# Query, key and value by seven block products instead of eight, with x parked in HBM and variances on ScalarE

## The chip, the cores and the metric

The kernel runs on one core of one Trainium2 chip. The metric is the device time of one execution in microseconds; the time before is the median of four runs, 3240.68 us (3240.06 to 3242.31).

## The reference, cut to what matters

Four graph layers work on `x` of shape (128, 128, 512): 128 batches of 128 nodes with 512 features, float32 throughout, with one weighted adjacency `adj` of 128 x 128. After each layer comes a residual addition and a normalisation over the features.

```python
x = layernorm(x + gnn0(x))   # (adj @ x) @ w0 + bias0
x = layernorm(x + gnn1(x))   # graph attention: h = x @ W, softmax(leaky(s1 + s2) * adj) @ h, elu
x = layernorm(x + gnn2(x))   # max over neighbours' features: relu(max(adj @ x) + b)
x = layernorm(x + gnn3(x))   # masked 8-head attention on x @ w_qkv, projection, o + layernorm(o)*gamma + beta
```

In layer 3 the queries, keys and values are `x @ w_qkv`, a 512 x 1536 product for each batch. `layernorm` has no gain of its own: (x - mean) / sqrt(var + 1e-5).

## The kernel before, in words

One batch is a tile `x` of 128 nodes (partitions) by 512 features. `batch(i)` is a generator that takes batch i through all four layers; each `yield use(engine, time, buffers)` asks a planner for an engine and for buffers, and the instructions that follow it are put into the program at that point. The planner (`Plan`) runs all chains against one another with estimated durations and fixes the order of the instructions on every engine: among requests that can start first it takes urgent ones, then the lowest rank, which is mostly the batch's number. It ends with the order; on the chip each engine runs its instructions in that order and waits on semaphores. PE requests that aren't urgent are planned up to 1 us after their inputs are ready (`MARGIN`).

The batches form groups: two pairs at the start, 28 groups of four, six pairs at the end. A group shares `xT` (its features transposed, 512 x up to 512 columns), `qkT` (queries and keys transposed, later the attention weights) and the layer 1 logits. Per batch, TensorE does:

- layer 0: `mixed_rows` (one 128x512 matmul with adj, L289) and `product` with w0 (four 128x512 matmuls, L262); the first 12 batches use `mixed` (L270)
- layer 1: `mixed` with the attention (L270) and `product` with W
- layer 2: one matmul with adj (L783)
- layer 3: `query_key` (L621) on the whole group's columns, `values` (a `product` into `v`, L262), `score` (L670, 64-row tiles, heads side by side), `attends` (L691), `product` with the projection (L262)

Each float32 matmul call becomes two instructions in the profile. `tiled` puts a group's scores and the attends of the group before it next to each other on PE; only the last groups have attends of their own (`attend`).

Transposes go through HBM: VectorE transposes 32x32 squares (L292, L798, L843), the SP queue writes them out (`to_squares`, `to_rows`) and reads them back in place (`from_squares`, `from_rows`); `features` brings a batch's columns into `xT` in this way. `layernorm_act` takes statistics on VectorE (`mean_rstd`: L191, L197, L199), the power -0.5 on GpSimd (`root`, L205) and applies it on ScalarE (L225); `layernorm_dve` applies it on VectorE (L230). `layernorm_sums` gets the mean from a sum that the operation before it left and the variance from a square with a sum on ScalarE (L239); only the last batch but one uses it. `pool_add` (L255) is an addition on GpSimd. `x` keeps its buffer, one of 19, from its load to the store of the result; PSUM has 8 banks (`ps`).

Of the kernel before, what the change touches and what calls it, by code (L numbers as in the profile page):

```python
# [8 lines left out]
F32 = mybir.dt.float32  # L9
AF = mybir.ActivationFunctionType  # L10
ALU = mybir.AluOpType
# [4 lines left out]
P = 128  # L16
D = 512
K = D // P
G = 4
FIRST, PAIRS = 2, 6  # L20
SOON = (0, 4, 0, 4, 10, 0)
WHOLE = 2
SCALED = 2
# [11 lines left out]
    "x": 19, "yT": 4, "z": 2, "e": 2, "et": 1, "eT": 2, "ex": 2, "xT": 2, "v": 7, "qkT": 2,  # L35
    "pt": 1, "xt": 2,
# [3 lines left out]
LATER = 18  # L40
LANDED = 4.0
MARGIN = 1.0
LAND, ROW_LAND = 2.0, 0.0053

# [96 lines left out]
def gnn_stack_kernel(  # L141
# [24 lines left out]
    one = ctx.enter_context(tc.tile_pool(name="one", bufs=1))  # L166
# [65 lines left out]
    def layernorm_sums(xb, total):  # L232
# [4 lines left out]
        b_sq = yield use("ACT", 1.2, "ex")  # L237
# [47 lines left out]
    def mixed_rows(xb, nodes):  # L285
# [4 lines left out]
        bt = yield use("DVE", 0.71, "xt", urgent=True)  # L290
# [59 lines left out]
    wqkv_sb = const.tile([P, K, 3 * D], F32, name="wqkv_sb")  # L350
    wproj_sb = const.tile([P, K, D], F32, name="wproj_sb")
# [11 lines left out]
    scalars_in, w0_in, w3_in, wa_ready = (Event() for _ in range(4))  # L363
# [16 lines left out]
    def loads():  # L380
# [44 lines left out]
        landing(w3_in, (4 * K + 3) * P)  # L425
        for i in range(12, NB):
            yield from load(i)
# [33 lines left out]

    def logit_rows(a_sb, slot):
# [3 lines left out]
        for s in range(2):  # L466
            for k in range(K):
                yield use("DVE", 0.8)
                scr = one.tile([P, D], F32, name="scr")
                nc.vector.scalar_tensor_tensor(  # L470
                    scr, w1_sb[:, k, :], 1.0, a_sb[:, s, :], op0=ALU.mult, op1=ALU.mult,
                    accum_out=wa[:, k, s : s + 1],
                )
        give(slot)
# [10 lines left out]
    class Group:  # L485


        def __init__(self, first, size):
            self.first, self.size = first, size
            self.chunks = D // (size * P)  # L490
# [3 lines left out]
            self.turned, self.qk = Event(size), Event(2 * K // self.chunks)  # L494
            self.rows, self.attended, self.scored = ([Event() for _ in range(size)] for _ in range(3))
            self.heads, self.o, self.sc = {}, {}, {}
            self.eT, self.xT, self.qkT, self.slot, self.left = {}, None, None, {}, {}
# [19 lines left out]
    def group(i):  # L517

        g = group_of[i]
        if g not in groups:  # L520
# [5 lines left out]
            steps = K // gr.chunks  # L526
            for n in range(2 * steps):
                plan.start(query_key(gr, n // 2 * gr.chunks + K * (n % 2)), rank + n / K)


            joined = len(sizes) - PAIRS
            if g < joined:
                plan.start(tiled(gr, groups.get(g - 1), range(size)), rank)
            else:
                plan.start(tiled(gr, None, range(size)), rank)
            if g >= joined - 1:
                for b in range(0, size, 2):
                    for bs in ((b, b + 1),) if g < len(sizes) - 1 else ((b,), (b + 1,)):
                        plan.start(attend(gr, bs), first)
# [3 lines left out]
    def attention1(gr, h):  # L543
# [5 lines left out]
        st = small.tile([P, 2, Q, S // Q], F32, name="s2")  # L549
# [58 lines left out]
    def query_key(gr, c):  # L608
        yield gr.turned
        yield w3_in  # L610
        got = yield use("PE", 3.44, lambda: ("ps",) if gr.qkT else ("ps", "qkT"), late=0.2)
        if gr.qkT is None:
            bp, gr.slot["qkT"] = got
            gr.qkT = buf(gr.slot["qkT"], G, 2 * K, P)
        else:
            bp = got
        n = gr.chunks
        p = bank(bp, n, gr.size * P)
        for j in range(n):
            for k in range(K):  # L620
                nc.tensor.matmul(  # L621
                    p[:, j, :], wqkv_sb[:, k, (c + j) * P : (c + j + 1) * P],
                    gr.xT[:, k, : gr.size * P], start=(k == 0), stop=(k == K - 1),
                )
        gr.read("xT", gr.size + 2 * K // n)
        yield use("ACT", 0.6, urgent=True)
        for j in range(n):
            dst = gr.qkT[:, : gr.size, c + j, :]
            if c < K:
                nc.scalar.mul(dst, p[:, j, :].rearrange("p (b n) -> p b n", b=gr.size), HD**-0.5)  # L630
            else:
                nc.scalar.copy(  # L632
                    dst.rearrange("p b (c r) -> p b c r", c=Q),
                    p[:, j, :].rearrange("p (b r c) -> p b c r", b=gr.size, c=Q),
                )
        give(bp)
        done(gr.qk)
# [46 lines left out]
    def attends(gr, bs, slots):  # L684
        for b, slot in zip(bs, slots):
            valued, prT = gr.heads.pop(b)

            p = bank(slot, K, P)
            for c in range(K):
                for j in range(2):  # L690
                    nc.tensor.matmul(  # L691
                        p[j * HD : (j + 1) * HD, c, :],
                        valued.v[:, (2 * c + j) * HD : (2 * c + j + 1) * HD],
# [3 lines left out]
            gr.o[b] = p, slot, valued  # L697
# [3 lines left out]
    def values(i, gr, event):  # L701
        b = i - gr.first
        yield gr.turned
        bp, bv = yield use("PE", 3.44, lambda: ("ps", "v"), late=0.2)
        p = product(
            bp, lambda k: gr.xT[:, k, b * P : (b + 1) * P], lambda k: wqkv_sb[:, k, 2 * D :]
        )
        yield use("ACT", 0.6, urgent=True)
        event.v = buf(bv, D)
        nc.scalar.copy(event.v, p)  # L710
        give(bp)
        gr.read("xT", gr.size + 2 * K // gr.chunks)
        event.slot = bv
        done(event)

    def features(xt, bt, gr, b):

        scratch = yield from to_squares(xt, bt)
# [287 lines left out]
```

## Time and profile before

| | |
|---|---|
| median of the runs | 3240.68 us |
| the profiled execution | 3240.78 us |
| its span | 3238.8 us, granted TensorE clock 0.999 |
| PE busy, instructions | 3225.0 us (100%), 12135 |
| DVE busy | 2627.0 us (81%) |
| ACT busy | 1183.1 us (37%) |
| POOL busy | 932.6 us (29%) |
| DMA | 366.15 MB, the SP queue's packets 39.6% of 16 engines' span |

PE is TensorE's matmuls, PEld its weight loads (they overlap), DVE is VectorE, ACT ScalarE, POOL GpSimd, SP the engine that issues the DMAs. Shares are of the span, first to last instruction; the time of the execution is 2.0 us longer. In groups of instructions, a group is a line, an operation and a tile, with count, busy time, mean length in ns, and the idle time before it with what ended that. "Busy" of pipelined matmuls counts overlapped time once, so it is the pitch from one to the next that is worked with, not the length of one.

### The profile page before, as it was taken

What the parts mean: (1) busy time and instruction counts of PE and PEld (TensorE: products, weight loads), DVE (VectorE), ACT (ScalarE), POOL (GpSimd) and SP (SyncE); (2) the same over time, 40 slices, a digit from 0 to 9 for tenths busy, and PEclk for the clock granted to TensorE, in tenths of its full rate; (3) what the DMA queues carried; (4) which work ended last, traced back from release to release, by engine and by line L of the source; (5) the groups of instructions that cost most, each with busy time, mean ns of one, the idle gap of its engine ahead of it and who ended that gap; (6) DMA issues with size and microseconds to landing.
All of it is one profiled execution on the core that took longest, in us unless ns stands there. A gap on an engine that the chain in (4) does not pass through costs nothing.

```text
span 3238.8 us, 40147 instructions
## 1 busy us (share of the span) xinstructions
PE 3225.0 (100%) x12135; PEld 1663.4 (51%) x12135; DVE 2627.0 (81%) x5649; ACT 1183.1 (37%) x3477; POOL 932.6 (29%) x1033
## 2 busy tenths in 40 slices
PE   9999999999999999999999999999999999999998
PEld 5654445545455454554544545545455454455565
DVE  7888777887878778888788787887878877888867
ACT  2444333333342333333334333343233332333432
POOL 3322222232332323323223232232322322323222
PEclk9999999999999999999999999999999999999999
DMA  6234333444334443344433444334443344442432
GB/s 217 77 103 120 108 97 93 135 122 127 87 93 134 123 127 99 88 129 120 128 96 91 127 122 129 108 78 124 123 128 111 87 110 129 127 121 71 126 89 98
DMA packets 732167, 366.15 MB, mean 113 GB/s; under 512 B 566192, under 2 KB 648496, under 8 KB 731952
## 3 DMA queue, kind: packets, MB, share of 16 engines
q1 hardware_dynamic: 731808, 363.33, 39.6%
q8 instruction: 97, 1.59, 0.2%
q14 instruction: 118, 0.97, 0.1%
q10 hardware_dynamic: 144, 0.26, 0.0%
HBM read 190.38 MB, written 173.08 MB: 112 GB/s over the span
## 4 chain that ended last, share of the span: by engine, by line
PE 98%; DVE 1%; DMA 1%; issue 0%; POOL 0%; SPq 0%; ACT 0%; POOLq 0%; DVEq 0%; ACTq 0%
PE ps L262 54%; PE ps L621 26%; PE ps L270 4%; PE ps L670 4%; PE ps L691 4%; PE ps L783 3%; PE ps L289 3%; DMA p_d<-pt 0%; DMA x_d<-xt 0%; DVE st L191 0%; PE ps L921 0%; DVE t L889 0%; DVE pt L843 0%; DMA yT<-x_d 0%; POOL rstd L205 0%
## 5 line engine op out<-in xcount | busy, mean ns | idle before, releaser
L621 PE MATMUL ps<-xT,wqkv_sb 128*128 128x512 f32 (+1 forms) x2304 | 886.0, 545 | 0.0
L205 POOL TENSOR_TENSOR rstd<-ve,neghalf 128x1 f32<-128x1 f32 x640 | 437.1, 683 | 1486.5 <-DVE ve L199 1250.6
L262 PE MATMUL ps<-w_sb,yT 128*128 128x512 f32 x1952 | 858.8, 592 | 1.8 <-DMA yT<-x_d 1.8
L621 PEld LDWEIGHTS ps<-xT,wqkv_sb 128*128 128x128 f32 x2304 | 437.7, 190 | 445.8 <-issue 416.1
L262 PEld LDWEIGHTS ps<-w_sb,yT 128*128 128x128 f32 x1952 | 369.9, 190 | 463.7 <-issue 445.4
L262 PE MATMUL ps<-wqkv_sb,xT 128*128 128x512 f32 x1024 | 448.2, 593 | 0.0
L262 PE MATMUL ps<-wproj_sb,v 128*128 128x512 f32 x1016 | 445.6, 595 | 0.7 <-ACT v L863 0.7
L833 ACT ACTIVATE qkT<-qkT,nmx 128x128 f32<-128x128 f32 x1008 | 389.1, 390 | 12.4 <-DVE nmx L819 12.4
L191 DVE BATCH_NORM_STATS2 st<-x 128x6 f32<-128x512 f32 x510 | 348.1, 683 | 38.4 <-ACT x L791 36.1
L255 POOL TENSOR_TENSOR x<-x,v 128x512 f32<-128x512 f32 x127 | 171.7, 1352 | 553.7 <-DVE v L882 552.9
L262 PEld LDWEIGHTS ps<-wqkv_sb,xT 128*128 128x128 f32 x1024 | 193.8, 190 | 240.6 <-issue 225.7
L262 PEld LDWEIGHTS ps<-wproj_sb,v 128*128 128x128 f32 x1016 | 190.8, 190 | 233.2 <-issue 227.2
L225 ACT ACTIVATE x<-x,nmr,rstd 128x512 f32<-128x512 f32 x257 | 204.2, 807 | 190.9 <-DVE nmr L223 189.1
L630 ACT ACTIVATE qkT<-ps 128x512 f32<-128x512 f32 (+1 forms) x144 | 77.4, 549 | 427.9 <-PE ps L621 424.8
L255 POOL TENSOR_TENSOR x<-x,beta_sb 128x512 f32<-128x512 f32 x128 | 166.2, 1300 | 233.4 <-DVE xt L798 218.2
L791 ACT ACTIVATE x<-x,mx 128x512 f32<-128x512 f32 x128 | 91.4, 718 | 335.8 <-DVE mx L789 331.0
L812 DVE TENSOR_TENSOR qkT<-ps,maskb 128x512 f32<-128x512 f32 x256 | 161.1, 682 | 45.5 <-PE ps L670 42.2
L771 ACT ACTIVATE ex<-ps 128x512 f32<-128x512 f32 x128 | 76.4, 597 | 328.1 <-PE ps L262 328.1
L843 DVE STREAM_TRANSPOSE pt<-qkT 128x1024 f32<-128x1024 f32 x128 | 158.2, 1236 | 41.8 <-DMA p_d<-pt 41.5
L755 DVE SCALAR_TENSOR_TENSOR scr<-x,wa_rows 128x512 f32<-128x512 f32 x256 | 183.0, 715 | 10.5 <-ACT x L225 5.9
L833 ACT ACTIVATION_READ_ACCUMULATOR qkT<-qkT,nmx 128x1 f32 x1008 | 191.2, 190 | 0.0
L632 ACT COPY qkT<-ps 128x512 f32<-128x512 f32 (+1 forms) x144 | 75.9, 539 | 298.0 <-PE ps L621 298.0
(91 smaller groups left out, 3612.7 us busy)
## 6 DMA issues: line engine op xcount, KB each, us to landing
p_d<-pt SPq DMA_DIRECT2D x128, 512.0 KB
qkT<-p_d SPq DMA_DIRECT2D x128, 512.0 KB
x_d<-xt SPq DMA_DIRECT2D x244, 256.0 KB
xT<-x_d SPq DMA_DIRECT2D x512, 64.0 KB
x<-in_x SPq DMA_DIRECT2D x127, 256.0 KB
out<-x SPq DMA_DIRECT2D x127, 256.0 KB
yT<-x_d SPq DMA_DIRECT2D x464, 64.0 KB
z<-s_d SPq DMA_DIRECT2D x64, 128.0 KB
```

The costliest lines, as they stand in the source:

```text
L191: nc.vector.bn_stats(st, src)
L205: nc.gpsimd.tensor_tensor(rstd, ve, neghalf, op=ALU.pow)
L225: nc.scalar.activation(xb, xb, AF.Identity, bias=nmr, scale=rstd)
L255: nc.gpsimd.tensor_tensor(dst, dst, other, op=ALU.add)
L262: nc.tensor.matmul(p, lhs(k), rhs(k), start=(k == 0), stop=(k == K - 1))
L270: nc.tensor.matmul(p[:, k, :], xb[:, k * P : (k + 1) * P], nodes, start=True, stop=True)
L621: nc.tensor.matmul(p[:, j, :], wqkv_sb[:, k, (c + j) * P : (c + j + 1) * P], gr.xT[:, k, : gr.size * P], start=(k == 0), stop=(k == K - 1),)
L670: nc.tensor.matmul(p[j][:, c, :], gr.qkT[rws, b, c, :], gr.qkT[rws, b, K + c, :], start=True, stop=True,)
L755: nc.vector.scalar_tensor_tensor(scr, xb, 1.0, wa_rows[:, j, :], op0=ALU.mult, op1=ALU.mult, accum_out=gr.s[:, b, j : j + 1],)
L812: nc.vector.tensor_tensor(pr[:, j * K : (j + 1) * K], sc[j], maskb[:, None, :].to_broadcast([P, K, P]), op=ALU.add,)
L833: nc.scalar.activation(pr[:, j, :], pr[:, j, :], AF.Exp, bias=nmx[:, j : j + 1], accum_out=sums[:, j : j + 1],)
L843: nc.vector.transpose(pt.rearrange("p c h s -> p h c s"), pr.rearrange("p h (c r) -> p h c r", c=Q))
```

## The change

**Seven block products.** Queries, keys and values are each a `section`. The group's transposed x is cut into four blocks (two feature halves by two halves of the batches), the weights into four (two feature halves by two output halves). On the weights, four sums are made once on GpSimd (`weight_sums`; two of them overwrite a block of the weights); on x, four differences a group on GpSimd (`gather`; one in place), so that `xT` has seven blocks. Seven products of blocks, each four matmul calls of 256 columns for a group of four, go into two or three PSUM banks: in one bank (`x`) four products are added up one after another, and ScalarE copies it out after each of the first three into `t` buffers (`keep`, `kept`) and after the fourth into place; VectorE adds such a copy to another bank (`add`, `added`), three times a section. `multiply` stands for the four matmul calls of one product. The query scale goes into the weights.

**Buffers.** `xT` has one buffer (of seven blocks) for two; `v` four (of two batches) for seven (of one). `xt`, `ex`, `scr` and `t1` now share five `t` buffers. `x` has 12 buffers for 19.

**x parked.** After layer 2's result has been transposed and beta3 added, `spill` stores x to HBM and frees its buffer; `fetch` reads it into one of two `xr` buffers once the batch has been attended. The last eight batches keep x where it is.

**Gather.** The reading of the transposed squares into `xT` moves from each batch (`features`) to one chain a group (`gather`), which waits for all its batches and for `xT`.

**Variances.** The norms of layers 0 and 1 and the last one all use `layernorm_sums`; the operation before each leaves the sum. Layer 2's norm and the inner norm of layer 3 stay.

**Attends apart.** `tiled` holds scores alone; each group's attends come in twos of their own.

The core of the diff:

```diff
 BUFS = {
     "ps": 8,
-    "x": 19, "yT": 4, "z": 2, "e": 2, "et": 1, "eT": 2, "ex": 2, "xT": 2, "v": 7, "qkT": 2,
-    "pt": 1, "xt": 2,
+    "x": 12, "xr": 2, "yT": 4, "z": 1, "e": 1, "et": 1, "eT": 3, "t": 5, "xT": 1, "v": 4,
+    "qkT": 2, "pt": 1,
 }
...
+    def weight_sums():
+        yield w3_in
+        yield use("POOL", 6.0)
+        nc.gpsimd.tensor_scalar(
+            wqkv_sb[:, :, :D], wqkv_sb[:, :, :D], HD**-0.5, None, op0=ALU.mult
+        )
+        for s in range(3):
+            for out, a, b, op in (
+                (S1, S3, A22, ALU.add), (S2, S1, A11, ALU.subtract),
+                (S3, A11, S3, ALU.subtract), (S4, A12, S2, ALU.subtract),
+            ):
+                yield use("POOL", 1.4)
+                nc.gpsimd.tensor_tensor(weight(s, out), weight(s, a), weight(s, b), op=op)
+        done(w3_ready)
...
-            steps = K // gr.chunks
-            for n in range(2 * steps):
-                plan.start(query_key(gr, n // 2 * gr.chunks + K * (n % 2)), rank + n / K)
-            joined = len(sizes) - PAIRS
-            if g < joined:
-                plan.start(tiled(gr, groups.get(g - 1), range(size)), rank)
...
+            plan.start(gather(gr), first)
+            for s in range(3):
+                plan.start(section(gr, s), rank + SECTION + (LATER if s == 2 else s / K))
+            plan.start(tiled(gr, None, range(size)), rank)
+            for b in range(0, size, ATTENDS):
+                bs = tuple(range(b, min(b + ATTENDS, size)))
+                for bs in (bs,) if g < len(sizes) - 1 else tuple((b,) for b in bs):
+                    plan.start(attend(gr, bs), first)
...
+    def gather(gr):
+        n = gr.half * P
+        for b in range(gr.size):
+            yield gr.squared[b]
+        landed = Event(gr.size)
+        for b in range(gr.size):
+            got = yield use("SP", 2.0, lambda: () if gr.xT else ("xT",))
...
+            from_squares(
+                gr.xT[:, 2 * j : 2 * j + 2, :, at : at + P].rearrange("p b k n -> p (b k) n"),
+                gr.scratch.pop(b),
+            )
+            done(landed, LANDED)
+        yield landed
+        yield w3_ready
+        for out, a, b in ((T3, B22, B12), (T1, B12, B11), (T2, B22, T1), (T4, B21, T2)):
+            yield use("POOL", 0.1 + 0.65 * gr.half)
+            nc.gpsimd.tensor_tensor(
+                gr.xT[:, out, :, :n], gr.xT[:, a, :, :n], gr.xT[:, b, :, :n], op=ALU.subtract
+            )
+        done(gr.summed)
+
+    def section(gr, s):
+        yield gr.summed
+        half, n = gr.half, gr.half * P
+        time = (0.9, 0.9, 0.86)[s] if half == 1 else 1.71
+        wide = 2 * n
...
+        x = bank(bx, D)[:, :wide]
+        multiply(x, A11, B11, True)
+        m1 = keep(x)
+
+        bz = yield use("PE", time, "ps", late=0.2)
+        z = bank(bz, D)[:, :wide]
+        multiply(z, A12, B21, True, True)
+        plan.start(release(add(z, m1, 0, 0), bz), gr.first)
+
+        yield m1[0]
+        yield use("PE", time, late=0.2)
+        multiply(x, S2, T2)
+        u2 = keep(x)
+
+        by = yield use("PE", time, "ps", late=0.2)
+        y = bank(by, D)[:, :wide]
+        multiply(y, S3, T3, True)
+        yield u2[0]
+        yield use("PE", time, late=0.2)
+        multiply(x, S1, T1)
+        u4 = keep(x)
+        c22 = add(y, u4, 1, 1)
+        yield u4[0]
+        yield use("PE", time, late=0.2)
+        multiply(x, S4, B22, final=True)
...
+        yield c22
+        yield use("PE", time, late=0.2)
+        multiply(y, A22, T4, final=True)
+        plan.start(release(add(y, u2, 1, 0), by), gr.first)
...
+    def spill(i, xb, biased, kept, spilled):
+        yield biased
+        yield use("SP", 0.5, late=2.5)
+        nc.sync.dma_start(kept, xb)
+        give(x_slot[i])
+        done(spilled)
+
+    def fetch(i, kept, spilled, fetched):
+        yield spilled
+        x_slot[i] = yield use("SP", 0.5, "xr", late=3.0)
+        xs[i] = buf(x_slot[i], D)
+        nc.sync.dma_start(xs[i], kept)
+        done(fetched)
...
     def batch(i):
         yield loaded[i]
         gr, xb = group(i), xs[i]
+        if group_of[i] >= RUN:
+            yield groups[group_of[i] - RUN].summed
...
-        nc.vector.tensor_tensor(xb, p, xb, op=ALU.add)
+        total = small.tile([P, 1], F32, name="total")
+        nc.vector.scalar_tensor_tensor(
+            xb, p, 1.0, xb, op0=ALU.mult, op1=ALU.add, accum_out=total
+        )
         give(bp)
-        yield from layernorm_act(xb)
+        yield from layernorm_sums(xb, total)
...
-        elif i >= NB - 1 - SCALED:
-            yield from layernorm_act(xb)
-        else:
-            yield from layernorm_dve(xb)
+        yield from layernorm_sums(xb, total)
```

## The prediction

> **What bounds the kernel now.** I read the page's busy times first, then its chain that ended last, then the waits of PE, then one period of PE's timeline. Part 1 and part 4 of the page:
>
> ```profile
> PE 3225.0 (100%) x12135; PEld 1663.4 (51%) x12135; DVE 2627.0 (81%) x5649; ACT 1183.1 (37%) x3477; POOL 932.6 (29%) x1033
> PE 98%; DVE 1%; DMA 1%; issue 0%; POOL 0%; SPq 0%; ACT 0%; POOLq 0%; DVEq 0%; ACTq 0%
> ```
>
> PE is busy for 3225.0 of 3238.8 us, and 98% of the chain runs through it. A busy PE could still hide waits, so I asked what PE waited for (engine, line and tile; total us, times, longest):
>
> ```profile
> PE ps L262 <- DMA yT<-x_d: 1.8, 1, 1.8
> PE ps L434 <- POOL ident masks.py:199: 1.4, 1, 1.4
> PE ps L262 <- ACT v L863: 0.7, 1, 0.7
> PE ps L921 <- ACT v L863: 0.7, 1, 0.7
> PE ps L262 <- DVE yT L276: 0.3, 1, 0.3
> ```
>
> That is 4.9 us of waiting; the rest of the idle time is the tail after the last matmul (3226.28 + 3.72 = 3230.0, so 8.8 us). So the time is matmul work laid end to end, and whatever removes matmul time counts in full as long as PE stays fed. In the timeline of PE, columns are start, length, line and shape; each call of matmul shows as two instructions:
>
> ```profile
> 1732.96 13.90 PE L262 MATMUL ps<-wqkv_sb,xT 128*128 128x512 f32 x32
> 1746.79 3.84 PE L670 MATMUL ps<-qkT 64*128 64x128 f32 x64
> 1750.56 3.71 PE L691 MATMUL ps<-qkT,v 128*64 128x128 f32 x64
> 1754.21 14.00 PE L262 MATMUL ps<-wproj_sb,v 128*128 128x512 f32 x32
> 1768.04 27.63 PE L621 MATMUL ps<-xT,wqkv_sb 128*128 128x512 f32 x64
> 1795.51 1.95 PE L270 MATMUL ps<-eT,x 128*128 128x128 f32 x16
> ```
>
> For a group of four batches q and k (L621) hold PE from 1768.04 to 1795.51, 27.47 us, or 0.4292 us an instruction; v takes 13.83 us (1732.96 to 1746.79). The same line starts again one period later, and a window of one period shows how full the others are (PE, PEld, DVE, ACT, POOL, then clock, DMA share, GB/s):
>
> ```profile
> 1667.60:1768.04 100.44, 100.44 (x369) 50.13 (x368) 81.83 (x177) 36.65 (x108) 29.17 (x33) 1.00 0.41 113
> ```
>
> **Matmuls removed.** Winograd's form does seven products of quarter-size blocks where the plain one does eight. It also halves the moving side: 256 columns, not 512. The pairs of batches at the end already run that shape, so its price is in the trace:
>
> ```profile
> 2973.48 13.98 PE L621 MATMUL ps<-xT,wqkv_sb 128*128 128x256 f32 x64
> 2987.30 1.95 PE L270 MATMUL ps<-eT,x 128*128 128x128 f32 x16
> 2989.08 1.02 PE L289 MATMUL ps<-x,adjT 128*128 128x512 f32 x2
> ...
> 3005.86 3.60 PE L262 MATMUL ps<-wqkv_sb,xT 128*128 128x512 f32 x8
> 3009.38 1.97 PE L691 MATMUL ps<-qkT,v 128*64 128x128 f32 x32
> 3011.28 3.70 PE L262 MATMUL ps<-wqkv_sb,xT 128*128 128x512 f32 x8
> 3014.82 3.60 PE L262 MATMUL ps<-wproj_sb,v 128*128 128x512 f32 x8
> ```
>
> 64 instructions of 256 columns take 13.82 us, 0.2159 each: half of 0.4292 and 0.6% more. 16 of 128 columns take 1.78 us, 0.111 each. A group of four: before 27.47 + 13.83 = 41.30; after 3 sections x 7 products x 8 instructions x 0.2159 = 36.27; saved 5.03, of which I keep 4.97 (v's 13.83 holds about 0.1 us of switching beyond 32 x 0.4292). A pair: before 13.82 + 16 x 0.4292 = 20.69; after 14 products of 8 x 0.111 = 12.43 and 7 of 4 x 0.2159 = 6.05; saved 2.2. There are 28 groups of four and 8 pairs: 28 x 4.97 + 8 x 2.2 = **157 us less on PE**.
>
> **Attends apart.** Before, four batches' scores and attends stand together: 1746.79 to 1754.21, 7.42 us, with about 0.2 us of changing tile shape around them. In the lines above two attends alone take 1.90 us, the product ahead of them 3.52 and the one behind 3.54, where one among its like takes 3.44: 2.08 us a pair. Two of these and 3.96 for four scores with their own edges make 8.12 against 7.6: 0.5 a group, 28 x 0.5 = **14 us more**.
>
> **Waits that the change adds to PE.** Inside a section three products wait for ScalarE to copy the same bank out before they accumulate on. The trace prices one uncovered hand-off at 0.74 us (product after copy L863, at the tail). Between bounds of 0 (other chains always fill, as in the window above, where PE is full) and 9 hand-offs x 36 groups x 0.74 = 240 us I take 8, some ten or so at the first and last group, where little else is ready. Everywhere else the cover is the other two sections and the group's other 60 us of matmuls (100.4 - 41.3, plus 0.5).
>
> **Beside PE.** These I cost at nothing, and name what is left over. Mean ns and counts are from the groups by line:
>
> ```profile
> L191 DVE BATCH_NORM_STATS2 st<-x 128x6 f32<-128x512 f32 x510 | 348.1, 683 | 38.4 <-ACT x L791 36.1
> L230 DVE TENSOR_SCALAR x<-x,mv,rstd 128x512 f32<-128x512 f32 x253 | 142.6, 565 | 3.2 <-POOL rstd L205 3.2
> L812 DVE TENSOR_TENSOR qkT<-ps,maskb 128x512 f32<-128x512 f32 x256 | 161.1, 682 | 45.5 <-PE ps L670 42.2 <-ACT v L710 2.9
> L239 ACT ACTIVATE ex<-x,nm 128x512 f32<-128x512 f32 x1 | 0.7, 722 | 1.9 <-DVE nm L236 1.9
> ```
>
> - DVE. Layers 0 and 1 lose statistics, aggregate, epsilon and bias (0.683 + 0.182 + 0.154 + 0.200) and gain 0.135 + 0.082 for the negated mean and the sum's read: 1.00 less, twice. The last norm loses 0.683 + 0.182 + 0.154 + 0.565 and gains the same 0.217: 1.37 less. 128 x 3.37 = 431 less. Added are 9 block sums a group: six at 0.682, three of k in halves at 2 x 0.42, 6.6 us; about 4.3 for a pair; 28 x 6.6 + 8 x 4.3 = 220 more. 2627 - 431 + 220 = 2416, 78% of the new span.
> - ACT. Per norm: square 0.722, its sum 0.186, epsilon 0.295, bias 0.295; three per batch and the last norm's 0.81: 128 x 5.3 = 679 more, and about 5 for k's halved copy. 1183 + 684 = 1867, 60%.
> - POOL. Four block differences a group at 1.30 (the row of the 128x512 addition), half-size at 0.72 for pairs: 28 x 5.2 + 8 x 2.9 = 169; the weight sums once, 12 x 1.30 and a scaling of four such widths, about 21. 933 + 190 = 1123, 36%. The weight sums start when the last weights land (a POOL wait ends on the projection weights at about 33 us) and the first q/k stands at 109.3, so they are hidden.
> - Queues. Parking adds 120 stores and 120 fetches of 256 KB, 63 MB to 363: the SP queue's 39.6% becomes at most 46%. SP issues them at 0.33 to 0.36 us (rows of loads and stores), some 85 us in all; before, SP waits over 600 us on final stores alone. Behind a fetch that waits for one of two buffers stand SP's next transfers (yT, probabilities); the spill waits for POOL's bias addition in the same way.
>
> A row on the POOL work: L894, with two SBUF operands, has median 751 ns but mean 912 and longest 1575; with L776, L889 and L755 the excess is about 60 us, beside 502 us of POOL's wide additions. 169 us more would stretch DVE by some 20 us, off the path. The Trainium skill, "SBUF — State Buffer", section "Who interferes with whom", speaks against it: a GpSimd operation that reads SBUF and a VectorE one with two SBUF inputs fully block each other. By that, if every difference blocked for its whole length, DVE would have 169 us more, an estimate of 2585 in all; the predicted time would be the same.
>
> **The sum.** 3238.8 - 157 + 14 + 8 = 3103.8 of span. The profiled execution took 3240.78, 2.0 above its span and level with the median of 3240.68: **3106**.
>
> **Rivals.**
> 1. Hand-offs uncovered. If one of three in each section stands open (the one after u4, which has no product of its own section between), 3 x 36 x 0.74 = 80 us on top of 3098: 3178. For: sections hold two or three of 8 banks each for long, and scores ask for six at once. Against: ACT has 40% free and the copies go ahead of other work.
> 2. Slower: the one xT buffer. Before there are two. Now a group's gather can't begin until the last section before it has read xT; then 16 transfers (11.4 us in the timeline of SP, 1743.46 to 1754.86), landing about 2 us, and four differences, 5.2: 18.6 us. The cover is 60 us of other matmuls, if their batches are ready with 12 x buffers for 19. The point where it decides is 143 / 36 = 4 us uncovered a group; with half uncovered, 28 x 9.3 = 260 more: 3358. Against: before, q/k starts 13 us after the gather's last issue, and the gather starts only 3.3 us ahead of the previous v's end (1746.79), so one buffer would shift it little.
> 3. No change: the gain of 143 is met by as much idle time from rivals 1 and 2 together; 3241.
>
> **How the numbers follow.** Forecast (3086 to 3135): 0.62. Its floor is 3240.8 - 157 with nothing added, 3084, its top 29 us of further hand-offs. Rival 1 (3135 to 3234): 0.18. No change, within 0.2% (6.5 us, about what measurement can tell): 0.03. Rival 2 and anything slower: 0.17. Faster is 0.62 + 0.18. The range leaves out the slower side and the top of rival 1: 3086 to 3210.
>
> **What would show it.** The profile after should have PE near 3085 busy with idle time of 15 to 25 us, 256-column instructions at 0.216, DVE near 2420, ACT near 1870, POOL near 1120, and a period near 96 us. Rival 1 shows as PE waits on ACT copies in the sections' line, rival 2 as PE waits on POOL's differences or on xT transfers. Wrong would be a 256-column pitch above 0.25 or DVE above PE.

## The result and the profile after

The changed kernel takes 3245.35 us (median of 42 runs, 3237.46 to 3251.60) beside 3241.11 us for the kernel before (60 runs): ratio 1.0011, 95% interval 1.0007 to 1.0016. That is within the 0.2% that the prediction called no change. It is 139 us above the predicted 3106 and 35 us above the top of the range. The profiled execution took 3244.35 us with a span of 3242.5 us.

Part 1 of the page after, and the view of the cores (span, mean granted clock of TensorE):

```profile
PE 3134.3 (97%) x14631; PEld 2084.0 (64%) x14631; DVE 2486.2 (77%) x5317; ACT 1773.8 (55%) x5182; POOL 1125.1 (35%) x1190
```

```profile
core 0: 3242.5 us, clock 0.984
```

PE has 91 us less busy time than before, and yet the span is 4 us longer: 108 us of it now are idle, where 13.8 were. The busy time itself holds something that the clock tells: before, it was 0.999. In the profile after, the trace grants half the clock in 19 stretches ahead of the last matmul. The view of these 19 windows together (their length, and PE's busy time in them) ends with:

```profile
sum 98.96, PE 76.81; mean PE 4.04
```

So half of 76.81, 38.4 us of PE's busy time, is lost to the clock. (Span x (1 - clock) would give 3242.5 x 0.016 = 51.9; the rest of it falls into PE's waits and behind the last matmul, where it costs nothing. Before, the only slow stretch lies behind the last matmul, from 3233.3 us on.) Busy time less this loss is the work of PE at full clock. With it the whole difference can be laid out, all terms from the two profiles (us):

| | before | after | difference | predicted |
|---|---|---|---|---|
| PE's work at full clock | 3225.0 | 3134.3 - 38.4 = 3095.9 | -129.1 | -157 + 14 = -143 |
| lost to the clock while PE is busy | 0.0 | 38.4 | +38.4 | none |
| PE's waits | 4.9 | 98.6 | +93.7 | +8 |
| other idle time, mostly the tail | 8.9 | 9.6 | +0.7 | none |
| span | 3238.8 | 3242.5 | +3.7 | -135 |

So the arithmetic was saved, within 14 us of what was predicted, and all of it was given back: some 70% as waits, 30% as a slower clock. PE's waits after (line, what it waited for, total us, times, longest us), the largest of them:

```profile
PE ps L855 <- DMA qkT<-p_d: 32.5, 13, 4.1
PE ps L686 <- ACT t L721: 12.0, 9, 2.1
PE ps L273 <- DMA yT<-x_d: 9.3, 2, 6.0
PE ps L281 <- DMA eT<-e_d: 7.7, 2, 5.4
PE ps L273 <- ACT yT L292: 7.6, 2, 5.6
...
PE ps L686 <- POOL xT L663: 1.6, 1, 1.6
```

These are 50 waits, 2 us each on the average (0.15 to 6.0), and no single bottleneck. The largest row is attends (L855) on the attention weights' way through HBM. Only 12.0 us are the sections' hand-offs (L686 on the kept copy L721), and only 1.6 us the gather's differences (L663).

How one such wait comes about can be followed between 305 and 330 us. The timeline of the SP queue (start, length, line, transfer, how many):

```profile
305.23 2.56 SPq L322 DMA_DIRECT2D yT<-x_d  x4
307.89 0.56 SPq L873 DMA_DIRECT2D x_s<-x  x1
308.58 2.56 SPq L322 DMA_DIRECT2D yT<-x_d  x4
311.51 0.33 SPq L336 DMA_DIRECT2D x_d<-t  x1
311.94 0.37 SPq L386 DMA_DIRECT2D x<-in_x  x1
312.41 1.61 SPq L336 DMA_DIRECT2D p_d<-pt  x1
...
318.50 0.33 SPq L336 DMA_DIRECT2D p_d<-pt  x1
...
323.23 0.37 SPq L340 DMA_DIRECT2D qkT<-p_d  x1
```

The timeline of VectorE in the same stretch:

```profile
307.80 1.23 DVE L1015 STREAM_TRANSPOSE pt<-qkT 128x1024 f32<-128x1024 f32 x1
...
317.23 1.25 DVE L1015 STREAM_TRANSPOSE pt<-qkT 128x1024 f32<-128x1024 f32 x1 [5.69 <-DMA p_d<-pt]
```

And PE's timeline there, with lines from three other places for comparison:

```profile
78.30 8.83 PE L273 MATMUL ps<-w_sb,yT 128*128 128x512 f32 x16 [1.91 <-ACT yT L292]
...
298.04 8.74 PE L273 MATMUL ps<-w_sb,yT 128*128 128x512 f32 x16 [6.02 <-DMA yT<-x_d]
...
327.25 1.97 PE L855 MATMUL ps<-qkT,v 128*64 128x128 f32 x16 [3.91 <-DMA qkT<-p_d]
329.15 3.41 PE L686 MATMUL ps<-xT,wsum_sb 128*128 128x256 f32 x8
...
796.94 1.99 PE L686 MATMUL ps<-xT,wsum_sb 128*128 128x256 f32 x8 [1.91 <-ACT t L721]
...
1739.17 7.03 PE L273 MATMUL ps<-wproj_sb,v 128*128 128x512 f32 x16
```

VectorE has transposed the weights into `pt` at 309.03, but their store stands behind the transfers of `yT` and goes out at 312.41. There is one `pt` buffer, so the next transpose waits 5.69 us for that store and stalls VectorE; its own store leaves at 318.50, comes back by the load at 323.23, and PE stands still for 3.91 us until 327.25. The four transfers of a batch take 2.56 us of the queue each time; the planner counts 2.0 for them (`use("SP", 2.0, ...)`).

The clock follows the waits. A product of 16 instructions takes 7.03 us undisturbed (at 1739.17), and 8.74 after a wait of 6.02 (at 298.04): 1.7 us more. A section's product of 8 takes 3.41 for the usual 1.89, right behind the attends that waited 3.91 us. Windows of 24 us of the profile after show it (PE, PEld, DVE, ACT, POOL busy, then the clock, the DMA share, GB/s):

```profile
264.00:288.00 24.00, 24.00 (x124) 14.61 (x124) 17.84 (x37) 9.26 (x21) 6.43 (x8) 1.00 0.36 80
288.00:312.00 24.00, 17.98 (x51) 10.06 (x50) 17.22 (x28) 12.16 (x59) 14.26 (x10) 0.86 0.75 175
312.00:336.00 24.00, 20.09 (x101) 16.30 (x100) 15.62 (x33) 12.10 (x35) 4.85 (x5) 0.86 0.71 214
```

Narrower windows show when it falls (PE busy, then the clock):

```profile
321.80:325.22 3.42, 1.54 (x19) 1.00 0.44 133
325.22:328.63 3.41, 1.38 (x14) 0.50 0.77 294
328.63:332.04 3.41, 3.41 (x13) 0.50 0.35 114
789.43:792.84 3.41, 1.58 (x8) 1.00 0.87 221
792.84:796.25 3.41, 1.96 (x8) 1.00 0.92 321
```

All changes of the clock in this profile lie on one grid of 3.413 us, and a slow stretch is one period of it (nine times) or two (ten times) at half clock. One began behind each period of full clock in which PE was idle for 1.88 us or more, as in the first of these lines (3.42 - 1.54), and behind none with 1.83 or less, as in the fourth (3.41 - 1.58). In the traces of the other runs the border lies between 1.83 and 2.01 us. So what counts is the idle time within one period: 19 of the 23 waits of 1.9 us or more were followed by a slow stretch, at 38.4 / 19 = 2.0 us of busy time each.

### The profile page after: what moved, and what is told of

Read it like the earlier page. It is cut to its first block, busy times and chain, and to the rows that moved or that the text cites. A ratio compares the mean times of both kernels' runs of the same rounds, so it can differ in the third digit from the quotient of the medians.

```text
span 3242.5 us, 47028 instructions
## 1 busy us (share of the span) xinstructions
PE 3134.3 (97%) x14631; PEld 2084.0 (64%) x14631; DVE 2486.2 (77%) x5317; ACT 1773.8 (55%) x5182; POOL 1125.1 (35%) x1190
## 3 DMA queue, kind: packets, MB, share of 16 engines
q1 hardware_dynamic: 766368, 426.26, 45.6%
## 5 line engine op out<-in xcount | busy, mean ns | idle before, releaser
L686 PE MATMUL ps<-xT,wqkv_sb 128*128 128x256 f32 (+1 forms) x2304 | 484.3, 357 | 0.0
L686 PEld LDWEIGHTS ps<-xT,wqkv_sb 128*128 128x128 f32 x2304 | 403.5, 191 | 80.9 <-issue 35.1
L686 PE MATMUL ps<-xT,wsum_sb 128*128 128x256 f32 (+1 forms) x1728 | 371.3, 360 | 6.8 <-ACT t L721 4.9
L686 PEld LDWEIGHTS ps<-xT,wsum_sb 128*128 128x128 f32 x1728 | 304.0, 192 | 82.2 <-issue 34.5
L721 ACT COPY t<-ps 128x512 f32<-128x512 f32 (+1 forms) x324 | 171.2, 532 | 233.6 <-PE ps L686 167.1
L663 POOL TENSOR_TENSOR xT<-xT 128x512 f32<-128x512 f32 (+1 forms) x144 | 177.8, 1235 | 292.2 <-DMA xT<-x_d 175.4
L250 ACT ACTIVATE t<-x,nm 128x512 f32<-128x512 f32 x263 | 188.5, 717 | 165.2 <-DVE nm L247 128.4
L686 PE MATMUL ps<-wqkv_sb,xT 128*128 128x256 f32 x1024 | 247.1, 382 | 0.0
L735 DVE TENSOR_TENSOR qkT<-ps,t 128x256 f32<-128x256 f32 (+1 forms) x324 | 178.4, 579 | 79.3 <-PE ps L686 42.3
L920 DVE SCALAR_TENSOR_TENSOR t<-x,wa_rows 128x512 f32<-128x512 f32 x256 | 205.6, 805 | 25.7 <-ACT x L260 16.4
L686 PEld LDWEIGHTS ps<-wqkv_sb,xT 128*128 128x128 f32 x1024 | 193.1, 191 | 48.9 <-issue 22.8
L266 POOL TENSOR_TENSOR xr<-xr,v 128x512 f32<-128x512 f32 x120 | 163.2, 1360 | 153.1 <-DMA xr<-x_s 61.9
```

Of the source, the lines that this page charges most:

```text
L250: nc.scalar.activation(buf(b_sq, D), xb, AF.Square, bias=nm, accum_out=squares)
L266: nc.gpsimd.tensor_tensor(dst, dst, other, op=ALU.add)
L663: nc.gpsimd.tensor_tensor(gr.xT[:, out, :, :n], gr.xT[:, a, :, :n], gr.xT[:, b, :, :n], op=ALU.subtract)
L686: nc.tensor.matmul(to, lhs, rhs, start=first and j == 0 and k == 0, stop=final and k == 1, skip_group_check=True,)
L721: nc.scalar.copy(held[1], p)
L735: nc.vector.tensor_tensor(c, a, b, op=ALU.add)
```

## The experiments

Theories after the result. **A**: the new order of the work lets PE run dry (with one `xT` and v in front, the put-off products that filled PE during a gather are gone), and each dry spell costs clock as well. **B**: the hand-offs inside the sections. **C**: transfers come late on a crowded SP queue, whose times the planner underrates. **D**: too few buffers (`xT`, `x`, `pt`). In every run that edits the order's makers, buffers or operations, the planner makes a new order; so a price below is that of an edit with the order that came out for it.

### The products in themselves: new_eight

The sections as eight plain block products, the rest of the change kept:

```diff
-        multiply(x, A11, B11, True)
-        m1 = keep(x)
...
+        for n_out, (i, j) in enumerate(((0, 0), (1, 0), (0, 1), (1, 1))):
+            slot = got if n_out == 0 else (yield use("PE", 2 * time, "ps", late=0.2))
+            p = bank(slot, D)[:, :wide]
+            multiply(p, ((A11, A12), (S3, A22))[i][0], (B11, B12)[j], True)
+            multiply(p, ((A11, A12), (S3, A22))[i][1], (B21, B22)[j], final=True)
+            plan.start(out(p, slot, i, j), gr.first)
```

> The new kernel with everything of the change but the seven products: each section forms its four blocks from eight plain block products, copied out by ScalarE, with no differences of x, no weight sums, no kept copies and no additions on VectorE. Theory A: the products are worth what the matmul rows said (8 against 7 products of 1.73 us, 3 x 1.73 a group of four, about 157 us), the dry stretches stay since buffers, gather and order of stages stay; about 3245 + 157 = 3400, with PE waits of 90 us or more and a clock below 0.99. Theory B: with the hand-offs gone PE is full again; 3241 + 14 for the separate attends = 3255, clock 0.999. Theory C: between, since the transfers stay: about 3350.

Measured: 3405.37 us, ratio to before 1.0506 (1.0490 to 1.0521). Part 1 of its page:

```profile
PE 3288.5 (97%) x15463; PEld 2222.8 (65%) x15463; DVE 2232.6 (66%) x4885; ACT 1783.6 (52%) x5290; POOL 925.3 (27%) x1034
```

Without differences, kept copies and their hand-offs there are still 115 us of idle time, for 108 in the changed kernel, and the time is 160 us longer. So the seven products are worth their predicted 157, each form in its own order, and bring no waits of their own that matter: B falls. What eats them is in the frame around them.

### Parts of the frame, in the kernel before: old_one_xT, old_apart, old_three, old_park

One `xT` for two:

```diff
-    ... "xT": 2, "v": 7, "qkT": 2,
+    ... "xT": 1, "v": 7, "qkT": 2,
```

> The kernel before with one xT buffer instead of two, nothing else. Theory A: a second xT lets v be put off (its rank is 18 later) into the next group's gather, and the 13.8 us of v per group fill PE there; with one buffer the gather must wait for v and PE runs dry once a group: 28 groups x 7 to 12 us, 3240 + 200 to 330, and the clock falls below 0.98, for another 50. Theory B and C: v has only to come earlier, 13 us of slack stand between the gather's last issue and the first q/k; within 20 us of 3241.

Measured: 3649.03 us, ratio 1.1262 (1.1245 to 1.1278), clock 0.952. PE's waits, first row:

```profile
PE ps L621 <- DMA xT<-x_d: 204.2, 23, 10.4
```

Here Rival 2 of the prediction stands in full. In this kernel v ranks far behind q and k (`LATER = 18`) and keeps `xT` long, which the changed kernel does not do; so this price is not the changed kernel's.

Attends in twos of their own:

```diff
-            if g < joined:
-                plan.start(tiled(gr, groups.get(g - 1), range(size)), rank)
...
+            plan.start(tiled(gr, None, range(size)), rank)
+            for b in range(0, size, 2):
+                for bs in ((b, b + 1),) if g < len(sizes) - 1 else ((b,), (b + 1,)):
+                    plan.start(attend(gr, bs), first)
```

> The kernel before with every group's attends in twos of their own instead of behind the next group's scores, nothing else. By the prediction's term 14 us more: 3255. Theory A: that term and up to 10 us of waits, since the attends now follow close on their transfers: 3255 to 3265. Theory C: the attends are where PE waits in the new kernel (39.9 us of 98.5), so most of it comes back here: 3285 or more, with waits of PE on the probabilities' transfers.

Measured: 3281.91 us, ratio 1.0126 (1.0111 to 1.0141), 40 us more. PE's busy time rose by 20.3 us (3225.0 to 3245.3) and its idle time by 17.9 (13.8 to 31.7). The prediction's term was 14, all of it busy time.

Both, with v ranked beside q and k (`LATER = 0`):

> The kernel before with three of the change's rules and none of its products, parking or variances: one xT buffer, v right with q and k (its rank no longer 18 later), attends in twos of their own. Theory A: v no longer holds the one xT, so less dry than with one xT alone (3649), but nothing fills the gather: 70 to 110 us of waits and a clock near 0.98 beside the attends' 14: 3330 to 3400. Theory C: the 3282 of separate attends, and 10 more.

Measured: 3361.52 us, ratio 1.0374 (1.0359 to 1.0390), 121 us more: a third of what one `xT` cost with v put off.

x parked after layer 2, 12 `x` and two `xr`:

```diff
-    "x": 19, "yT": 4, ...
+    "x": 12, "xr": 2, "yT": 4, ...
...
+        if i < NB - 8:
+            kept = dram.tile([P, D], F32, name="x_s", bufs=24)
+            plan.start(spill(i, xb, biased, kept, spilled), i)
```

> The kernel before with x parked in HBM after layer 2 and fetched for the last sum, as in the change, with 12 x and 2 xr buffers for 19 x. The prediction's price was nothing: 3241. Theory A: fewer batches in flight leave PE dry now and then, 40 to 50 us of waits and 15 of clock: 3300. Theory C: 240 more transfers on the SP queue; the waits are on transfers that land late (yT, probabilities), 3290 or more, with SP's queue full where PE waits.

Measured: 3303.02 us, ratio 1.0188 (1.0173 to 1.0204), 62 us more; PE's waits, first rows:

```profile
PE ps L691 <- DMA qkT<-p_d: 25.6, 4, 18.0
PE ps L270 <- DMA eT<-e_d: 8.9, 8, 3.3
```

18.0 us of the first row are one wait near the end (3260 to 3278 us). Neither row is the parked x itself; whether its transfers or the order with fewer buffers make the others late was not separated. The prediction's price for it was nothing.

### Parts of the frame, in the changed kernel: new_joined, new_stats

Attends joined again behind the next group's scores, as before:

```diff
-            plan.start(tiled(gr, None, range(size)), rank)
...
+            if g < joined:
+                plan.start(tiled(gr, groups.get(g - 1), range(size)), rank)
```

> The new kernel with each group's attends put back behind the next group's scores. If separate attends cost it what they cost the old kernel (3282 - 3241 = 40 us), it comes to 3205. Theory A: with one xT the next group's scores come only after its whole gather and sections, so the attends and projections that could fill PE in that stretch are put off beyond it: 3300 to 3400, clock below 0.98.

Measured: 3381.85 us, ratio 1.0434 (1.0417 to 1.0452), clock 0.967. Separate attends, which cost 40 us in the kernel before, are worth 137 in the changed one.

Variances of layers 0 and 1 and of the last norm on VectorE again:

```diff
-        yield from layernorm_sums(xb, total)
+        yield from layernorm_act(xb)
...
-        yield from layernorm_sums(xb, total)
+        yield from layernorm_dve(xb)
```

> The changed kernel with the variances of layers 0 and 1 and of the last norm taken on VectorE again, by the sums, as in the kernel before; the rest as in the changed kernel. By the terms of the prediction VectorE goes from 2486 to about 2917 us, 90% of the span, and ScalarE falls by some 200 to 300 us. The prediction priced this move at nothing, since VectorE's work lay beside PE's: 3245. By the remainder of the runs so far (three edits of the kernel before +121, parking +62, products -160, attends in the first of these; sum +23, measured +4) the move gained about 19 us: 3264. If VectorE so full delays the kept copies and sums of the seven products, each of which PE waits for: 3290 to 3350, with new waits of PE on VectorE's added copies or the sections' q and k.

Measured: 3364.77 us, ratio 1.0380 (1.0359 to 1.0401), clock 0.974: above the highest of the three values expected. Part 1 of its page and the first row of PE's waits:

```profile
PE 3167.8 (94%) x14631; PEld 2095.2 (62%) x14631; DVE 2896.9 (86%) x6083; ACT 1181.7 (35%) x3523; POOL 1133.9 (34%) x1190
```

```profile
PE ps L855 <- DMA qkT<-p_d: 65.9, 19, 16.2
```

VectorE at 86% of the span is not the bound, and no large wait of PE ends on it; but the weights that it transposes come late, and the attends' waits double from 32.5 to 65.9 us (16.2 of them in one wait near the end). The new waits that the expectation named are small: in the sections 3.6 us on added copies (L686 on L735), and 19.2 for 12.0 on the kept ones. The prices do not add up: +121 and +62 in the kernel before, -160 for the products and -119 for the variances make -96, where the whole change measures +4. The sum leaves out the smaller buffers and the gather as one chain, and edits can act on one another; it shows only that a price holds for the kernel and the order in which it was measured.

### Clock alone: new_warm

Identity transposes put where the planner saw PE idle for over 0.7 us, to keep the clock up:

```diff
+                gap = t - self.free.get("PE", 0.0)
+                if gap > 0.7 and t > 20.0:
+                    self.warm(gap)
...
+        for k in range(int(gap / 0.25)):
+            nc.tensor.transpose(p[:, k % K, :], ident, ident)
```

> The new kernel with idle transposes of the identity put into a free PSUM bank wherever its order lets PE stand for over 0.7 us, one per 0.25 us of the gap; nothing else moves. Theory A (the order runs PE dry, 98.5 us of waits, and after long waits the TensorE clock falls, which costs another 1.6% of 3134 us, 52 us): most waits are filled, the clock comes back from 0.984 to 0.994 or more, and the time falls by 25 to 45 us to about 3210, although no useful work is added or removed. Theory B (PE waits for hand-offs inside the sections; the clock only shows it): same waits, no change beyond 10 us. Theory C (transfers land late on a crowded SP queue): the waits come where the order expects none, so the transposes miss them; no change beyond 10 us.

Measured: 3241.09 us, ratio 1.0000 (0.9990 to 1.0010): 4 us below the changed kernel, a miss for A and within what B and C had given. PE's waits fell to 63.5 us and the clock rose to 0.991, half way back, but PE's busy time rose as well, to 3161.1 us with 351 more instructions: filling takes PE's time too, and where the planner sees idle time is not quite where the chip has it. So this run does not show what the clock is worth.

### The order alone: new_order, new_order2, new_queue, new_ranks

The instructions, buffers and transfers of the changed kernel; only ranks, start rules (`RUN`, `PACE`), the grouping of attends and the planner's constants differ. The first try:

```diff
-SOON = (0, 4, 0, 4, 10, 0)
+SOON = (2, 2, 2, 4, 8, 0)
-ATTENDS = 2
-RUN = 6
-SECTION = 2
-PACE = 0
-EAGER = 8
+ATTENDS = 4
+RUN = 8
+SECTION = 0
+PACE = 23.0
+EAGER = 12
-LAST, AHEAD = 14, 4
+LAST, AHEAD = 14, 2
-LATER = -0.1
+LATER = 0.3
-MARGIN = 1.0
+MARGIN = 0.8
...
+            yield early(i) - 6
```

> The new kernel with the same instructions, buffers and transfers in another order: only ranks and start rules of the planner change (the first matmul of layer 0 ranks 6 batches earlier, its product 8 later, so that products of later batches stand ready while a group's xT is filled; some constants with it). Theory A (the order lets PE run dry, and the clock falls after it): waits of PE fall from 98.5 to about 50 us, the clock rises to 0.992 or more, 3245 - 50 - 25 = 3170 (3140 to 3190). Theory C (late transfers on the SP queue) and theory D (12 x and 5 t buffers are too few): the same transfers and buffers, so 3245 within 15.

Measured: 3212.68 us, ratio 0.9916 (0.9901 to 0.9931). A direct sign for A, though 43 us short of what was expected: PE's waits stayed at 89.5 us, of which one of 16.4 near the end; more of the gain came by the clock, 0.990. A queue delay like the one shown above was at the root of the one that was followed: four transfers of `yT` took 3.27 us, and VectorE then waited 5.83 us for `pt`. Hence the second try, with the queue's four transfers counted at their measured length:

```diff
-ATTENDS = 2
-RUN = 6
-SECTION = 2
+ATTENDS = 4
+RUN = 30
+SECTION = -2
-LAST, AHEAD = 14, 4
-LATER = -0.1
-LANDED = 4.0
-MARGIN = 1.0
+LAST, AHEAD = 10, 4
+LATER = 0.3
+LANDED = 4.5
+MARGIN = 1.5
-        b1 = yield use("SP", 2.0, "yT", late=LANDED)
+        b1 = yield use("SP", 2.6, "yT", late=LANDED)
-            got = yield use("SP", 2.0, lambda: () if gr.xT else ("xT",))
+            got = yield use("SP", 2.6, lambda: () if gr.xT else ("xT",))
...
+            yield early(i) - 10
```

> The changed kernel with the same instructions, buffers and transfers in another order: the planner counts four transfers of the queue at 2.6 us, as the traces of the changed kernel show them (2.54 to 2.6), and not at 2.0; it takes a margin of 1.5 us ahead of a batch in place of 1.0; layer 0's small matmuls rank ten batches earlier; v ranks 0.3 later and not 0.1 earlier; the ranks of sections, runs and attends are shifted. Theory A (the order lets PE run dry) with C (the planner's times for the queue are too short, so that what it takes as ready is late): PE's waits fall from 98 to about 60 us and the clock comes back to 0.992, so 3165 to 3185. If the order of new_order already gives all that an order can give, and the rest comes from buffers (theory D): 3205 to 3220, waits 90 to 95. If the order does not matter and new_order was a lucky one: 3245.

Measured: 3151.50 us (3151.16 to 3153.82), ratio 0.9724 (0.9709 to 0.9738): better than both kernels, and 14 us below the range expected. The cores view, part 1 of the page, and all rows of PE's waits over 2 us:

```profile
core 0: 3152.0 us, clock 0.993
```

```profile
PE 3096.4 (98%) x14631; PEld 2074.1 (66%) x14631; DVE 2485.8 (79%) x5317; ACT 1765.0 (56%) x5182; POOL 1125.6 (36%) x1190
```

```profile
PE ps L855 <- DMA qkT<-p_d: 17.2, 4, 15.9
PE ps L686 <- ACT t L721: 12.4, 5, 4.8
PE ps L273 <- ACT yT L292: 6.2, 2, 5.6
PE ps L957 <- ACT x L260: 4.6, 4, 1.9
PE ps L686 <- DMA xT<-x_d: 2.9, 2, 1.8
```

The same number of instructions on every engine, and the same busy time on VectorE within 0.4 us; PE's waits are 46.9 us for 98.6, of them 15.9 in one piece near the end (3113 to 3129 us), on the attention weights' way through HBM. The sections' hand-offs are where they were, 12.4 us: apart from that piece they are the largest part of what the order did not remove. In the two stretches of time in which the changed kernel's clock fell to 0.86, PE is now full:

```profile
288.00:312.00 24.00, 24.00 (x91) 16.31 (x90) 19.68 (x37) 19.27 (x56) 12.00 (x13) 1.00 0.61 193
312.00:336.00 24.00, 24.00 (x142) 17.98 (x141) 19.89 (x47) 11.30 (x25) 10.39 (x11) 1.00 0.48 165
```

Is it the queue's count (C) or the ranks and margins (A without C)? Each alone. The first is the two lines of 2.6 above, the second everything above but those two lines; it keeps `LANDED` at 4.5 for 4.0, a time of transfers too, so the parting of A from C is not quite clean.

> The changed kernel with one part of new_order2 alone: the planner counts four transfers of the queue at 2.6 us, as the traces show them, and not at 2.0; ranks and margin stay as in the changed kernel. If the planner's times for the queue are what makes the changed kernel dry (theory C): most of the 94 us of new_order2 come with this alone, 3150 to 3190, and PE's waits on the attends' and aggregations' transfers shrink from 60 us to 20 or 30. If it is the ranks and the margin (theory A without C): 3225 to 3250, with waits as before.

> The other part of new_order2: its ranks and its margin of 1.5 us, with the queue's four transfers counted at 2.0 us as in the changed kernel. Theory A without C: 3150 to 3170, as new_order2. Theory C: 3215 to 3245, the gain gone with the count. If both are parts: this and new_queue each lie between 3170 and 3225, and their gains add up to about 94 us.

Measured: the count alone 3199.52 us, ratio 0.9867 (0.9853 to 0.9882); the ranks and margins alone 3196.95 us, ratio 0.9864 (0.9848 to 0.9881). The gains over the changed kernel are 45.8 and 48.4; their sum is 94.2, and both together measured 93.9. PE's waits on attends of the one and the other:

```profile
PE ps L855 <- DMA qkT<-p_d: 23.0, 10, 8.6
```

```profile
PE ps L855 <- DMA qkT<-p_d: 22.9, 8, 5.1
```

So both are parts, of equal size, and each gains in two ways, about half by fewer waits (77.4 and 72.2 us in all, for 98.6) and most of the rest by the clock (0.991 and 0.990). The expectation that C alone would bring most of the 94 us was missed. So was its way there: the waits on the attends' and aggregations' transfers were 40.2 us in the changed kernel, not the 60 that it names, and with the count alone they are 23.0; but those on `yT` rose from 9.3 to 17.0, and PE's waits on transfers of all kinds are 42.4 us for 49.5. D is not needed for the 94 us. Which parts of the change (one `xT`, 12 `x`, separate attends) spoiled the first order stays open; the prices in the kernel before say only that each can. The kernel before has 13.8 us of idle time in all, so another order of its own could gain little by fewer waits. Whether a second `xT` or `pt` would take more was not tried, and how far an order's time scatters with any small edit of its constants isn't known: four orders of the changed kernel gave 3152 to 3213 us beside its own 3245, but they were chosen, not drawn.

## Why the prediction was wrong

- **What bounds the kernel** was read rightly, and so was its condition: whatever removes matmul time counts in full "as long as PE stays fed". The prediction then took it that PE would stay fed because before it was; but the 4.9 us of waits before were the property of one order, and the change made another, with 98.6.
- **Matmuls removed**, 157, and the 256-column price of 0.2159 us held: eight instructions take 1.73 us from one product to the next (308.34 to 310.06 in PE's timeline, 0.216 each), PE's work at full clock fell by 129 against 143 with the attends' term, and new_eight puts the products at 160.
- **Attends apart**, 14, was too small: 20 us of busy time in old_apart, and 18 of idle time that was not priced.
- **Waits that the change adds to PE** is the step that failed: 8 us, measured 94. It looked for them at the hand-offs inside the sections, where they are indeed 12 (nine, at 1.3 us each for the 0.74 that it took); the other 87 stand at attends, aggregations and products whose inputs come late through the queue or from busy engines. The bounds of 0 to 240 around it held them, and the value was taken near the wrong end, because the window of one full period before was taken as cover for an order that no longer was.
- **The clock** was no term of the sum: 38 us. Before there were no waits long enough to show the drop (the longest was 1.8 us); waits and clock should have been priced together, here at about 1.4 times the waits ((93.7 + 38.4) / 93.7).
- **Beside PE.** The amounts were good: DVE 2416 predicted and 2486 measured (of the 70, L920 took 205.6 us for L755's 183.0, and L1012 174.7 for L840's 158.9, both longer beside more GpSimd work; the prediction's other estimate of 2585, every difference blocking VectorE for its whole length, was too high), ACT 1867 and 1774, POOL 1123 and 1125, DMA at most 46% and 45.6%. The conclusion "at nothing" was not: parking cost 62 us in the kernel before, and the variances' move, taken at nothing too, is worth 119 in the changed one. An engine at 77% with a queue in its loop is no cover without end.
- **Rivals.** The time is that of the third, "as much idle time from rivals 1 and 2 together", but its causes are small here: 12.0 us on copies (1) and 1.6 on the differences, nothing on `xT`'s transfers (2). What came in their place is the order as a whole with a mistimed queue. Rival 2's point of decision, 4 us uncovered a group, was nearly met in sum, (93.7 + 38.4) / 36 = 3.7, at other places.
- With another order of the same instructions the change is worth 2.8% (0.9724). The forecast of 3106 is 45 us below that; of the step that failed, 46.9 us of waits and a clock of 0.993 are left, and whether an order without them exists is not known.

## What to carry to other kernels

Where one engine is busy for 99.6% of the span under one fixed order, an edit that removes its work also removes that order: price the idle time that the planner's stale ranks and durations will leave, and compare the old and the new arithmetic inside one frame (here seven against eight products) before judging it. After such an edit, set the planner's durations from the new trace, above all those of queues that now carry more, and tune the ranks again; here that was worth 94 us of the 139 by which the forecast was missed. Count a dry spell of TensorE at its length plus what the clock takes behind it.

## What the hardware showed unexpectedly

- Behind 19 of the 23 waits of 1.9 us or more TensorE runs at half clock for 3.41 or 6.83 us (part of it in the wait itself), and the next product loses about 1.7 us, no matter whether the wait was 1.91 us (8.83 us for 7.03, at 78.30) or 6.02 (8.74, at 298.04). What decides is whether more than about 1.9 us of idle time falls into one period of the grid of 3.413 us: after a wait of 1.91 us at 796.94 the next product took 1.99 us for 1.89, and a wait of 2.29 us at 1188.10, split by the grid into 0.68 and 1.61, cost nothing. The clocks of the kernels here roughly go with their waits, from 0.999 (4.9 us of waits) through 0.993 (46.9) and 0.984 (98.6) to 0.952, where one `xT` left PE idle for 327 us; new_eight has 0.988 with 105.6.
- The Trainium skill, "TensorE: Matmul & The Clock Gate", section "What's actually happening", gives half the clock after an idle window of about 3.4 us, in a window that runs freely. A free-running period of 3.41 us is what this trace shows too. But by the length of that window only 8 of the 50 waits could have cost anything, an estimate of 8 x 1.7 = 14 us; the trace has 19 slow stretches and 38.4 us, so here it differs: about 1.9 us of idle time within a period is enough.
- The four transfers of one batch's squares, 64 KB each, hold the SP queue for 2.56 us in the stretch shown, and for 3.27 in the one followed in new_order; a store or load of 256 KB as one transfer holds it there for 0.33 to 0.56. Yet all of SP's issues together take 1156 of 3242 us in the changed kernel, and its packets only 45.6% of the engines' span. So the queue is not full on the average: its transfers go out in order, and what stands behind a row of fours, or behind a transfer that itself waits, comes late. The first row of SP's own waits (total us, times, longest):

```profile
SPq L1076 <- ACT xr L260: 279.6, 82, 14.7
```
